# Layer 0 of a four-layer attention kernel: the next queries' norm in two steps on VectorE, three context steps ahead of cross attention's first pass, and two smaller staging tiles

## The chip, the cores and the metric

The kernel runs on one core of one Trainium2 chip. The metric is the device time of that core in microseconds (us): the median of three timed runs. One more run was taken with the hardware profiler; all times of single instructions come from it. Lines are told as L317, which is line 317 of the kernel before. Engines have the profile's names: PE is TensorE (PEld its weight load), DVE is VectorE, ACT is ScalarE, POOL is GpSimd, SP is the queue that issues the DMAs.

## The reference

Four layers work on x, 8 sequences of 256 tokens with 320 features, and on a context of 8 x 120 tokens with 192 features. The change lies in layer 0, and in the preparation of context keys and values for layers 1 to 3. Layer 0 is, cut to what matters:

```python
def attention(x, ctx, Wq, Wk, Wv, Wo, bo, heads):          # 20 heads of 16
    q, k, v = fq_sym(x @ Wq), fq_sym(ctx @ Wk), fq_sym(ctx @ Wv)   # 8-bit steps, one step for the whole tensor
    w = fq_zero(softmax(q k^T * dh ** -0.5))                       # 8-bit steps, one step for the whole tensor
    return (w v) @ Wo + bo

x = x + attention(layer_norm(x, ln1), layer_norm(x, ln1), Wq1, Wk1, Wv1, Wo1, bo1)   # self
x = x + attention(layer_norm(x, ln2), ctx, Wq2, Wk2, Wv2, Wo2, bo2)                  # cross
x = x + geglu_ff(layer_norm(x, ln3))
```

A quantisation step is taken from the maximum over a whole tensor (all batches), so each attention needs two passes over the scores: the first finds the sums of the softmax and from them the step of the weights, the second computes the weights again, rounds them to whole steps and multiplies them with the values. Layers 1 and 2 have cross attention to the same context with weights of their own, layer 3 too.

## The kernel before, in words

x stays in SBUF. A batch is one sequence of 256 tokens, as two tiles of 128. Heads go in groups, four heads to a group, and a "round" of the second pass handles one or two groups of a batch: five rounds make a batch.

The order of the work is written out by hand: generators are advanced in turn by `weave` (L651; each part has a round at which it starts), and `paced` (L663) lets a generator take a step only in every second round. Each engine then has one queue, in an order that the scheduler of the framework settles from this program order, from dependences and from its own estimate of times; an engine runs its queue strictly in that order. `behind` (L288) adds an order edge between two instructions of one engine, without a semaphore.

Self attention's second pass is `s.out_all()` (L1535). In each round, `weights` (L1565) calls `exps` (L1437): PE computes the scores of four heads into two PSUM pairs (L1454), ACT takes the exponential of each (L1461, tile `e`), and DVE rounds each to whole steps (L1569, tile `w`, from `e`). `e` and `w` share five buffers, so an exponential may have to wait for a rounding of the round before. PE multiplies the weights with the values two rounds later (L1551), DVE scales the result (`oTq`, L1561), and in two further rounds `project_out_steps` (L476) multiplies with Wo on PE (L120), after POOL has added the bias to x (`xb`, L481), and DVE adds the product into x (`x_sb`, L487). Meanwhile POOL rounds the values of the next batch (`whole_v`, L1355: `tv` at L1360, a memset at L1363, copies at L1369 and L1373).

Woven into this, from round 8 on, runs `c.queries_all()` (L1282): as soon as a batch of x is finished, its norm is taken (`normed`, L300: statistics, mean and variance, `ve` at L312 on DVE; rstd by a power at L314 on POOL; the two x-hat instructions at L317, one for each tile of 128 tokens), the result is transposed on PE (L334) and copied out by ACT with the norm's factors (`xT`, L342), and three matmul groups (L120) give cross attention's queries `Q`. In batches 1 to 6 the x-hat instructions are on POOL (`on=nc.gpsimd`), in batches 0 and 7 on DVE.

Cross attention begins with the quantisation steps (`c.steps()`), the rounding of the first batch's queries and keys (`c.whole(0, True)`, L1330), and then the first pass: `tops_all` (L1395) computes scores (L1410) in six units for each batch, and DVE takes their negated maximum (`negm`, L1413); `sums_all` follows two units behind the batch with exponentials and sums; `whole_all` rounds the next batch's queries and keys on POOL.

Woven into the first pass is `ahead`, which is `context_steps` (L702): 4 steps that compute layer 1's context keys for two batches each (`keys`, L754; PE 12 matmuls at L730, ACT copies them out into the staging tile `kst` at L364 and L368, and two DMAs write them to DRAM), then 4 steps of values (8 matmuls each, staging tile `vst`), then the same for layers 2 and 3. PSUM pairs for scores and for context steps come from the same pool of three. One step, with the loads of its weights, is taken right at the start, one after `c.steps()`, and up to 20 in the weave, one in two rounds; what is left runs beside the second pass of cross attention.

Of the kernel before, what the change touches and what calls it, by code (L numbers as in the profile page):

```python
# [11 lines left out]
F32 = mybir.dt.float32  # L12
BF16 = mybir.dt.bfloat16
AF = mybir.ActivationFunctionType
# [4 lines left out]
P = 128  # L19
B, N, C = 8, 256, 320  # L20
NT = B * N // P
TPB = N // P
# [11 lines left out]
G = H * PAD // P  # L34
# [3 lines left out]
G3 = H3 * PAD3 // P  # L38
T3 = 4
K3 = M - T3  # L40
# [14 lines left out]
class Kernel:  # L55
# [221 lines left out]
    def weight_o2(self, pool, name):  # L277
# [7 lines left out]
                    self.nc.sync.dma_start(w[r : r + D, g], src[h * D : (h + 1) * D])  # L285
        return w

    def behind(self, ins, last):  # L288

        if last is not None:  # L290
            order = mybir.DependencyInfo(mybir.DependencyClass.NoSync, mybir.DependencyReason.DATA)
            self.tc.add_manual_dep(ins.ins, last.ins.name, order, reason="order on the engine")
# [4 lines left out]
    def bank(self):  # L297
        return self.ps_a.tile([P, 512], F32, tag="a", name="pa")

    def normed(self, b, ln, on=None):  # L300

        nc = self.nc
        x = self.x[:, TPB * b : TPB * (b + 1), :]
        if ln is None:
            return x
        mv = self.small.tile([P, TPB, 2], F32, tag="mv", name="mv")
        for t in range(TPB):
            st = self.small.tile([P, 6], F32, tag="bnst", name="bnst")
            nc.vector.bn_stats(st, x[:, t, :])
            nc.vector.bn_aggr(mv[:, t, :], st)  # L310
        ve = self.small.tile([P, TPB], F32, tag="ve", name="ve")
        nc.vector.tensor_scalar(ve, mv[:, :, 1], EPS, None, ALU.add)  # L312
        rstd = self.small.tile([P, TPB], F32, tag="rstd", name="rstd")
        nc.gpsimd.tensor_tensor(rstd, ve, self.nhalf, ALU.pow)  # L314
        xh = self.work.tile([P, TPB, C], F32, tag="xh", name="xh")
        for t in range(TPB):
            (on or nc.vector).tensor_scalar(  # L317
                xh[:, t], x[:, t], mv[:, t, 0:1], rstd[:, t : t + 1], ALU.subtract, ALU.mult
            )
        return xh  # L320

    def turned(self, x, dst, at, ln=None, singles=False):

# [378 lines left out]
    def context_steps(self):  # L702
# [18 lines left out]
        wk = lambda n: weight("ck", n)  # L721
        wv = lambda n: weight("cv", n, 2)
        half = lambda i: slice(64 * i, 64 * (i + 1))

        def both(outs, whole, halves, more=False):

# [27 lines left out]
        def keys(name, w, k0, k1):  # L754
            k = k1 - k0
            for b in range(0, B, 2):
                ps = self.pair()
                keys_to(ps, w, ((0, (0, 1)), (2 * k, (2,))), slice(b, b + 2), k0, k1)
                st = pool.tile([P, 2, G, k], F32, tag="ks", name="kst")
                pv = ps[:, :, : 4 * k].rearrange("p i (m b k) -> p i m b k", m=2, b=2)  # L760
                for i in range(2):
                    self.put_k(st[:, i], pv[:, :, 0, i], pv[:, 0, 1, i])
                    nc.sync.dma_start(self.kd[name][:, b + i, :, k0:k1], st[:, i])
                yield

        w, w2 = wk("L1_xattn_k2"), wv("L1_xattn_v2")
# [24 lines left out]
        ps = self.pair()  # L791
        n = B * NIP
        keys_to(ps, w, ((0, (0, 1)), (n, (2,))), slice(0, B), NTXT, M)
        st = pool.tile([P, G, n], F32, tag="ks", name="kst")
        self.put_k(st, ps[:, :, :n], ps[:, 0, n : 2 * n], 1)
        for b in range(B):
            nc.sync.dma_start(self.kd["both"][:, b, :, NTXT:], st[:, :, b * NIP : (b + 1) * NIP])
# [12 lines left out]
        for b in range(0, B, 2):  # L810
            ps = self.pair()
            keys_to(ps, w, ((0, (0, 1)), (2 * K3, (2, 3))), slice(b, b + 2), 0, K3)
            st = pool.tile([P, 2, G3, K3], F32, tag="ks", name="kst")
            pv = ps[:, :, : 4 * K3].rearrange("p i (g b k) -> p g i b k", g=2, b=2)
            for i in range(2):
                for g in range(2):
                    nc.scalar.activation(
                        st[:, i, 2 * g : 2 * g + 2], pv[:, g, :, i], AF.Identity,
                        bias=self.cols[:, COL_ONE + 2 : COL_ONE + 3],
                    )  # L820
                nc.sync.dma_start(self.kd["last"][:, b + i], st[:, i])
            yield


# [361 lines left out]
class Quant:  # L1186
# [95 lines left out]
    def queries_all(self):  # L1282

        k, nc, w = self.k, self.k.nc, self.w
        x, xT = {}, {}

        def norm(b):
            x[b] = k.normed(b, self.ln, on=nc.gpsimd if 0 < b < B - 1 else None)

        def turn(b):  # L1290
            xT[b] = k.work.tile([P, 3, N], F32, tag="xT", name="xT")
            k.turned(x.pop(b), xT[b], 0, self.ln)
            self.q[b] = self.pool.tile([P, 3 * N], F32, tag="Q", name="Q", bufs=B)

        def project(b, m):
            ps = k.pair()
            k.mm(ps[:, 0, :N], [(w["q"][:, c, m * P : (m + 1) * P], xT[b][:, c, :]) for c in range(3)])
            nc.scalar.copy(self.q[b][:, m * N : (m + 1) * N], ps[:, 0, :N])
            if m == 2:
                self.top(0, b, self.q[b])  # L1300

        todo = {0: norm, 3: turn, 6: lambda b: project(b, 0), 7: lambda b: project(b, 1), 8: lambda b: project(b, 2)}
        for r in range(5 * B + 4):
            for b in range(B):
                if r - 5 * b in todo:
                    todo[r - 5 * b](b)
            yield
# [227 lines left out]
    def out_all(self):  # L1535

        k, nc, kc, ks = self.k, self.k.nc, self.kc, self.ks
        st = {}
        groups = [gs for gs, h in self.units if h == 0]
        rounds = len(groups)  # L1540

        def values(b, gs, w):
            for n, g in enumerate(gs):
                if g in (0, 4):
                    st["o"] = k.bank()
                o = st["o"]
                at = g // 2 % 2 * N
                for c in range(kc):
                    for j in range(4):
                        i = (n * kc + c) * N  # L1550
                        nc.tensor.matmul(  # L1551
                            o[j * PAD : (j + 1) * PAD, at : at + N], self.v[b][:ks, c, k.head(g, j), :],
                            w[:ks, j, i : i + N], start=g in (0, 4) and c == 0, stop=g in (3, 4) and c == kc - 1,
                            skip_group_check=True,
                        )
                if g in (3, 4):
                    if g == 3:
                        st["oT", b] = k.work.tile([P, 3, N], F32, tag="oT", name="oTq", bufs=1)
                    oT = st["oT", b]
                    dst = oT[:, :2, :] if g == 3 else oT[:, 2:, :]  # L1560
                    nc.vector.tensor_scalar(  # L1561
                        dst.rearrange("p c n -> p (c n)"), o[:, : dst.shape[1] * N], self.sc[:, 14:15], None, ALU.mult
                    )

        def weights(b, gs):  # L1565
            es, n = self.exps(b, gs, range(4), 1)
            w = self.pool.tile([P, 4, 512], BF16, tag="e", name="w", bufs=5)
            for i, e in enumerate(es):
                nc.vector.tensor_scalar(  # L1569
                    w[:ks, 2 * i : 2 * i + 2, :n], e[:ks, :, :n], MAGIC, MAGIC, ALU.add, ALU.subtract  # L1570
                )
            return w

        def project(b):
            yield from k.project_out_steps(b, st.pop(("oT", b)), self.w["o"], self.brow)

        for _ in self.whole_v(0):
            pass
        self.shift(0)
        todo, projects = [], {}  # L1580
        for r in range(rounds * B + 4):
            b, i = divmod(r, rounds)
            if b < B:
                w = weights(b, groups[i])
                if i == 0:
                    more = self.whole_v(b + 1) if b + 1 < B else iter(())
                todo.append((b, groups[i], w))
            if len(todo) > (2 if b < B else 0):
                values(*todo.pop(0))

            for t in range(TPB):
                d, left = divmod(r - 2 - t, rounds)
                if left == 0 and 1 <= d <= B:
                    if t == 0:
                        projects[d] = project(d - 1)
                        next(projects[d])
                    next(projects[d], None)
            if b < B:
                for _ in range(2):
                    next(more, None)  # L1600
                if i == rounds - 2 and b + 1 < B:
                    self.shift(b + 1)
            yield
# [3 lines left out]
def kernel(ctx: ExitStack, tc: tile.TileContext, a, out):  # L1607
    k = Kernel(ctx, tc, a, out)
    with ExitStack() as es:
# [15 lines left out]
        with tc.tile_pool(name="l0", bufs=1) as pool:  # L1625
# [24 lines left out]
            brow["ff0"] = k.bias_row(k.fk, 2)  # L1650
            w["self"], brow["self"] = load("L1", "q1", "k1", "v1", "o1_w", 3)
            c.steps()
            next(ahead)
            for _ in c.whole(0, True):
                pass
            n = len(c.units)
            k.weave(
                (0, c.tops_all()), (n + 4, c.sums_all()), (0, c.whole_all()), (5, v),
                (1, k.paced(islice(ahead, 20), 1)),
            )  # L1660
            c.weight_steps()

# [127 lines left out]
```

## Time and profile before

| | us |
|---|---|
| median of three timed runs | 2206.34 |
| the three runs | 2202.88, 2206.34, 2210.78 |
| the profiled run | 2212.34 |
| span of the profiled run, first to last instruction | 2210.5 |
| PE busy in it | 2041.3 (92%) |
| DVE, ACT, POOL busy in it | 1122.6, 822.9, 360.3 |
| self attention's second pass with the queries woven in | 257 to 412 |
| start of cross attention | 412 to 445 |
| cross attention's first pass | 445 to 543 |

Lines of the timeline are: start, duration, engine, line and operation, out<-in, shapes, xN for N instructions shown as one, and in brackets the idle time ahead of it on its engine with what ended it. The table by stretch gives busy time (and instructions) of each engine, then the granted clock of PE as a share of full speed, the DMA share and GB/s.

### The profile page before, as it was taken

Reading aid. Unit: us, or ns where it says so; the run is one execution under the profiler, and the core shown is the slowest. Engines: PE = TensorE matmul, PEld = TensorE weight load, DVE = VectorE, ACT = ScalarE, POOL = GpSimd, SP = SyncE. Lnnn points to the kernel's source line nnn. Section 1 sums busy time; section 2 is a strip of 40 time slices with the busy share of each in tenths; the row PEclk is TensorE's granted clock in tenths of the full one; section 3 lists DMA queues with packets and bytes.
Section 4 is the critical chain, followed back from the end, with each engine's and each line's share of the span. In section 5 each row is a group of like instructions: output and inputs, shape, how many; then the busy total and the mean of one; then the engine's idle time right before and its main releaser. Section 6 shows DMA issues by size and latency. Waiting matters only on the chain.

```text
span 2210.5 us, 38239 instructions
## 1 busy us (share of the span) xinstructions
PE 2041.3 (92%) x16413; PEld 1197.1 (54%) x16413; DVE 1122.6 (51%) x1695; ACT 822.9 (37%) x1249; POOL 360.3 (16%) x366
## 2 busy tenths in 40 slices
PE   6888889898899999999999999899999999999997
PEld 5643345554444555455555555545555655666664
DVE  4388687555742221335556566621121566546565
ACT  3347878467532121124444434321101333222221
POOL 1192056621411000000000010100000100000100
PEclk9989889899989999999999999999999999999999
DMA  4000000642111000020000001100000120000000
GB/s 118 17 12 2 1 1 1 172 112 57 55 47 51 1 0 1 1 93 2 2 2 22 27 25 36 46 2 0 0 1 1 24 64 26 18 18 26 23 19 16
DMA packets 79303, 63.21 MB, mean 29 GB/s; under 512 B 48410, under 2 KB 68318, under 8 KB 78622
## 3 DMA queue, kind: packets, MB, share of 16 engines
q1 hardware_dynamic: 75070, 57.06, 9.3%
q10 hardware_dynamic: 4064, 3.71, 0.6%
q8 instruction: 129, 2.11, 0.4%
q14 instruction: 40, 0.33, 0.1%
HBM read 42.61 MB, written 17.37 MB: 27 GB/s over the span
## 4 chain that ended last, share of the span: by engine, by line
PE 74%; DVE 17%; ACT 4%; issue 3%; DMA 1%; POOL 0%; ACTq 0%; SPq 0%; DVEq 0%; POOLq 0%
PE pf L588 13%; PE pf L120 13%; PE pf L132 9%; PE pa L120 7%; PE pa L451 6%; PE pf L434 4%; PE pa L588 3%; PE pf L139 3%; DVE negm L1413 3%; PE pf L389 3%; DVE rs L459 3%; PE pf L730 3%; PE pf L1454 2%; PE pa L1476 2%; DVE negm L396 2%
## 5 line engine op out<-in xcount | busy, mean ns | idle before, releaser
L440 ACT ACTIVATE e<-pf 128x1024 f32<-128x1024 f32 (+2 forms) x176 | 158.4, 945 | 219.2 <-PE pf L434 212.2
L396 DVE TENSOR_REDUCE negm<-pf 128x4 f32<-128x1024 f32 (+4 forms) x224 | 188.0, 885 | 97.1 <-PE pf L389 97.1
L588 PE MATMUL pf<-xTf,ff 128*128 128x512 f32 x512 | 232.5, 601 | 5.2 <-DVE negm L396 5.2
L459 DVE RECIPROCAL rs<-pa 128x256 f32<-128x256 f32 x88 | 152.2, 1745 | 143.6 <-PE pa L451 143.6
L1461 ACT ACTIVATE e<-pf,sc_s 128x1024 f32<-128x1024 f32 x160 | 169.4, 1117 | 55.0 <-PE pf L1454 45.8
L481 POOL TENSOR_TENSOR xb<-x_sb,brow 128x640 f32<-128x640 f32 x40 | 62.3, 1557 | 775.5 <-DVE x_sb L487 734.6
L613 DVE SCALAR_TENSOR_TENSOR hT<-pf,cols_sb,gl 128x512 f32<-128x512 f32 x64 | 47.9, 750 | 256.8 <-ACT gl L612 254.5
L1413 DVE TENSOR_REDUCE negm<-pf 128x4 f32<-128x1024 f32 (+2 forms) x128 | 143.4, 1133 | 63.5 <-PE pf L1410 56.7
L120 PE MATMUL pf<-ff,hT 128*128 128x320 f32 x640 | 174.4, 434 | 0.0
L588 PEld LDWEIGHTS pf<-xTf,ff 128*128 128x128 f32 x512 | 94.9, 191 | 125.3 <-issue 119.4
L120 PEld LDWEIGHTS pf<-ff,hT 128*128 128x128 f32 x640 | 120.9, 190 | 55.5 <-issue 6.1
L612 ACT ACTIVATE gl<-pf,cols_sb 128x512 f32<-128x512 f32 x64 | 43.9, 687 | 249.6 <-PE pf L588 249.6
L389 PE MATMUL pf<-kT,qT 32*128 32x120 f32 (+1 forms) x1920 | 111.8, 324 | 18.8 <-ACT e L440 18.5
L434 PE MATMUL pf<-qT,kT 32*128 32x256 f32 (+1 forms) x1280 | 119.8, 405 | 9.1 <-DVE negm L396 7.5
L120 PE MATMUL pa<-o,oT 128*128 128x320 f32 x352 | 105.7, 441 | 15.2 <-DVE oT L460 15.2
L1454 PE MATMUL pf<-Q,K 32*128 32x256 bf16 (+1 forms) x960 | 91.3, 294 | 24.7 <-DVE negm L1413 14.1
L389 PEld LDWEIGHTS pf<-kT,qT 32*128 32x128 f32 x1920 | 82.0, 185 | 59.1 <-ACT e L440 28.1
L641 POOL TENSOR_TENSOR xb<-x_sb,brow 128x640 f32<-128x640 f32 x16 | 25.2, 1575 | 542.6 <-DVE x_sb L646 527.9
L451 PE MATMUL pa<-e,v 128*32 128x256 f32 (+1 forms) x1280 | 105.6, 390 | 2.3 <-ACT e L440 1.7
L1569 DVE TENSOR_SCALAR w<-e 128x1024 bf16<-128x1024 f32 (+2 forms) x128 | 87.4, 692 | 32.1 <-ACT e L1461 31.0
L132 PE MATMUL pf<-xT,q 128*128 128x256 f32 x384 | 100.5, 391 | 0.4 <-ACT e L440 0.2
L1461 ACT ACTIVATE e<-pf,sc_c 120x1024 f32<-120x1024 f32 (+1 forms) x96 | 88.5, 981 | 31.6 <-PE pf L1454 28.8
(284 smaller groups left out, 3436.3 us busy)
## 6 DMA issues: line engine op xcount, KB each, us to landing
ff<-in_L_xattn_Wff_dram SPq DMA_DIRECT2D x1, 2560.0 KB
qT<-nT SPq DMA_DIRECT2D x160, 4.0 KB
ff<-in_L_xattn_ff_w_dram SPq DMA_DIRECT2D x1, 2560.0 KB
out_dram<-x_sb SPq DMA_DIRECT2D x16, 160.0 KB
kd_cross<-kst SPq DMA_DIRECT2D x8, 300.0 KB
vd_cross<-vst SPq DMA_DIRECT2D x8, 300.0 KB
vd_both<-vst SPq DMA_DIRECT2D x8, 300.0 KB
kT<-kd_cross SPq DMA_DIRECT2D x8, 300.0 KB
```

Of the source, the lines that this page charges most:

```text
L120: self.nc.tensor.matmul(out, l, r, start=i == 0, stop=i == len(pairs) - 1)
L132: self.nc.tensor.matmul(o, *t[c], start=start and c == 0, stop=stop and c == n - 1, skip_group_check=True)
L389: nc.tensor.matmul(s[j // 2][:, j % 2, o : o + nk], qT[r : r + PAD, g, t * P : (t + 1) * P], kT[r : r + PAD, g, :nk], start=True, stop=True,)
L396: nc.vector.tensor_reduce(negm[:, n, 2 * i : 2 * i + 2, g0 : g0 + len(gs), :].rearrange("p j g t -> p j (g t)"), sv[:, :, :, k0:k1], AX.X, ...
L434: nc.tensor.matmul(s[j // 2][:ks, j % 2, o : o + N], kT[r : r + PAD, g, c * ks : (c + 1) * ks], qT[r : r + PAD, g, :], start=True, stop=True,)
L440: nc.scalar.activation(e[:ks, 2 * i : 2 * i + 2, :n], s[i][:ks, :, :n], AF.Exp, scale=scale)
L451: nc.tensor.matmul(o[j * PAD : (j + 1) * PAD, what * N : (what + 1) * N], w, es[g][:ks, j, c * N : (c + 1) * N], start=first and c == 0 an ...
L459: nc.vector.reciprocal(rs, o[:, N:])
L588: ins = nc.tensor.matmul(*args, **kw)
L1413: nc.vector.tensor_reduce(negm[:, 2 * h : 2 * h + 2, gs[0] : gs[-1] + 1, :].rearrange("p j g t -> p j (g t)"), s[:, :, : len(gs) * TPB * n ...
L1454: nc.tensor.matmul(s[at // 2][:ks, at % 2, o : o + N], l, m, start=not shift and o == 0, stop=shift and o + N == n, skip_group_check=True,)
L1461: nc.scalar.activation(e[:ks, :, :n], ps[:ks, :, :n], AF.Exp, scale=self.sc[:ks, 9:10])
```

## The change

Three edits.

A. `normed` is split: `norm_steps` is a generator that first takes the statistics and rstd, and at its next step makes the two x-hat instructions, always on DVE. `queries_all` takes the two steps in rounds 5b and 5b + 1 of a batch. The x-hat of the first tile gets an order edge behind the last rounding `w` that has been written at that point (`k.last_w`); the x-hat of the second tile gets none. In the compiled order of DVE this gives, for batches 1 to 6: `ve`, x-hat of the second tile, `w`, `w`, x-hat of the first tile, `oTq`; for batch 0: `w`, x-hat, `w`, x-hat, where before it was x-hat, x-hat, `w`, `w`.

B. After `c.steps()` three context steps are taken instead of one, so the steps with keys 2, 3 and 4 of layer 1 are written ahead of cross attention's first scores; the weave takes 18 instead of 20. On PE 12 + 12 matmuls at L730 move ahead of the first L1410, and the later context steps move up by two places.

C. The staging tile for keys held both batches of a step in one buffer; now each batch has a tile of its own out of two buffers. Each batch's DMA was its own before, too.

```diff
@@ def normed
-    def normed(self, b, ln, on=None):
+    def normed(self, b, ln):
...
+        steps = self.norm_steps(b)
+        next(steps)
+        return next(steps)
+
+    def norm_steps(self, b):
+
+        nc = self.nc
+        x = self.x[:, TPB * b : TPB * (b + 1), :]
...
         nc.gpsimd.tensor_tensor(rstd, ve, self.nhalf, ALU.pow)
+        yield
         xh = self.work.tile([P, TPB, C], F32, tag="xh", name="xh")
         for t in range(TPB):
-            (on or nc.vector).tensor_scalar(
+            self.last_norm = nc.vector.tensor_scalar(
                 xh[:, t], x[:, t], mv[:, t, 0:1], rstd[:, t : t + 1], ALU.subtract, ALU.mult
             )
-        return xh
+            if t == 0 and self.norm_behind is not None:
+                self.behind(self.last_norm, self.norm_behind)
+        yield xh
@@ def context_steps
+        staged = lambda g, n: pool.tile([P, g, n], F32, tag="ks", name="kst", bufs=2)
...
-                st = pool.tile([P, 2, G, k], F32, tag="ks", name="kst")
                 pv = ps[:, :, : 4 * k].rearrange("p i (m b k) -> p i m b k", m=2, b=2)
                 for i in range(2):
-                    self.put_k(st[:, i], pv[:, :, 0, i], pv[:, 0, 1, i])
-                    nc.sync.dma_start(self.kd[name][:, b + i, :, k0:k1], st[:, i])
+                    st = staged(G, k)
+                    self.put_k(st, pv[:, :, 0, i], pv[:, 0, 1, i])
+                    nc.sync.dma_start(self.kd[name][:, b + i, :, k0:k1], st)
...
@@ def queries_all
+        def stats(b):
+            x[b] = k.norm_steps(b)
+            next(x[b])
+
         def norm(b):
-            x[b] = k.normed(b, self.ln, on=nc.gpsimd if 0 < b < B - 1 else None)
+            k.norm_behind = k.last_w
+            x[b] = next(x[b])
+            k.norm_behind = None
...
-        todo = {0: norm, 3: turn, 6: lambda b: project(b, 0), 7: lambda b: project(b, 1), 8: lambda b: project(b, 2)}
+        todo = {0: stats, 1: norm, 3: turn, 6: lambda b: project(b, 0), 7: lambda b: project(b, 1), 8: lambda b: project(b, 2)}
@@ def weights in out_all
-                nc.vector.tensor_scalar(
+                k.last_w = nc.vector.tensor_scalar(
                     w[:ks, 2 * i : 2 * i + 2, :n], e[:ks, :, :n], MAGIC, MAGIC, ALU.add, ALU.subtract
                 )
@@ tile_xattn_kernel
             c.steps()
-            next(ahead)
+            for _ in range(3):
+                next(ahead)
             for _ in c.whole(0, True):
                 pass
...
-                (1, k.paced(islice(ahead, 20), 1)),
+                (1, k.paced(islice(ahead, 18), 1)),
```

The third use of the staging tile, layer 3's keys, is split in the same way.

## The prediction, made before the changed kernel was run

> **What bounds the kernel now.** I read the chain of work that ended last, then the busy table by stage, then the engine timelines of the two places that the change touches. All times are of the profiled execution: span 2210.5 us, run 2212.34 us, which is 6.0 us above the median of the three timed runs (2206.34; 2202.88 to 2210.78). The chain:
>
> ```profile
> PE 74%; DVE 17%; ACT 4%; issue 3%; DMA 1%; POOL 0%; ACTq 0%; SPq 0%; DVEq 0%; POOLq 0%
> ```
>
> TensorE (PE) bounds the kernel, GpSimd (POOL) has no share. The stages are self attention's second pass (257 to 412), the start of cross attention (412 to 445) and its first pass (445 to 543):
>
> ```profile
> 257.00:412.00 155.00, 135.81 (x1290) 81.33 (x1289) 117.93 (x231) 115.42 (x151) 75.91 (x68) 0.89 0.12 31
> 412.00:445.00 33.00, 24.84 (x152) 13.65 (x152) 16.73 (x27) 11.89 (x42) 33.00 (x29) 0.74 0.57 165
> 445.00:543.00 98.00, 93.29 (x1044) 48.13 (x1043) 47.46 (x88) 71.49 (x119) 10.75 (x8) 0.98 0.35 85
> ```
>
> Columns: stretch, length, busy PE, weight loads, VectorE, ScalarE, GpSimd, granted clock, DMA. The first pass is PE's (93.29 of 98). Its start is not: there PE has gaps and a clock of 0.74.
>
> **Part A, the norm.** Batches 1 to 6 lose two GpSimd x-hats (L317) and gain two on VectorE; batches 0 and 7 were on VectorE already. In the steady stretch a batch takes 15.6 us (x_sb at 333.30, then 348.90), of which PE is busy 14.12, ScalarE 13.5, GpSimd 12.4, VectorE 12.08. GpSimd, VectorE and ScalarE around one norm, each from its own timeline:
>
> ```profile
> 338.99 1.16 POOL L314 TENSOR_TENSOR rstd<-ve,nhalf 128x2 f32<-128x2 f32 x1
> 340.25 3.42 POOL L317 TENSOR_SCALAR xh<-x_sb,mv,rstd 128x320 f32<-128x320 f32 x2
> 343.66 1.22 POOL L1360 TENSOR_SCALAR tv<-V,sc_s 128x640 f32<-128x640 f32 x1
> ```
>
> ```profile
> 338.04 0.88 DVE L312 TENSOR_SCALAR ve<-mv 128x2 f32<-128x2 f32 x1
> 338.82 1.28 DVE L1569 TENSOR_SCALAR w<-e 128x1024 bf16<-128x1024 f32 x2
> ```
>
> ```profile
> 339.52 2.12 ACT L1461 ACTIVATE e<-pf,sc_s 128x1024 f32<-128x1024 f32 x2 [0.24 <-PE pf L1454]
> ```
>
> What is removed bought nothing on the path: GpSimd ends x-hat at 343.66, and the transposes that read it start at 343.96 without a wait. What is added lies on the path. In the compiled order of the changed kernel only the first tile's x-hat is held behind the weight roundings w; the second tile's has no such edge and stands right behind ve, ahead of both w. So VectorE's queue stops there for rstd, with the two w behind it, and the exponential whose buffer the first w frees (the second of the 2.12 pair, due at 339.52 + 1.12 = 340.64) behind those; PE's next scores wait for that exponential.
>
> How late is the first w? rstd alone takes 0.715 us (shortest of eight; 1.16 beside w): 338.99 + 0.71 = 339.70. From there GpSimd goes straight to tv (L1360) and the memset (L1363). Batch 0 of before shows such a meeting:
>
> ```profile
> 290.09 0.79 POOL L1360 TENSOR_SCALAR tv<-V,sc_s 128x640 f32<-128x640 f32 x1
> 290.94 1.22 POOL L1363 MEMSET V<- 128x1280 bf16 x1
> ```
>
> ```profile
> 290.13 2.22 DVE L317 TENSOR_SCALAR xh<-x_sb,mv,rstd 128x320 f32<-128x320 f32 x2 [0.61 <-POOL rstd L314]
> 292.27 1.37 DVE L1569 TENSOR_SCALAR w<-e 128x1024 bf16<-128x1024 f32 x2
> ```
>
> The x-hat pair took 2.22 us there, against 0.80 us in batch 7, where GpSimd had nothing to do; its end, 292.35, lies just behind the memset's, 292.16. [...] By this row the first w ends 339.70 + about 2.6 (tv 0.8, memset 1.2, the rest of w 0.5) = 342.3, 1.7 us past 340.64. By the uncontended row it ends 338.92 + 0.78 (rstd) + 0.44 (x-hat) + 0.69 (w) = 340.87, 0.2 late. I take 1.7: it is the same pair of instructions beside the same x-hat. ScalarE runs almost without gap from 339.52 until PE's only wait of the period (1.25 us for xT), so nothing absorbs it.
>
> Sum of A: batches 1 to 4 have tv and memset there: 4 x 1.7 = 6.8 (0.8 by the other end). Batch 5 has none: 0.2. Batch 6: 0, since its first w ends at 387.5 either way by the wait on the residual row. Batch 7: 0, same engine and a PE-bound tail. Batch 0 gains: there both w stood behind both x-hats, PE waited 3.6 us and ScalarE 4.6 us for the first; now it goes ahead (2.4 earlier) and the second 0.9 earlier. I take -1.5, between -2.4 and 0. Stall: **+5.5** (-1.4 to +7).
>
> The clock. Granted clock goes down in steps of 3.41 us, and one such stretch after 636.76 to 640.17 fell to half although PE's longest gap in it was 0.76 us: it held almost only 32-row matmuls (L1454, L1551). A stretch with 1.54 us idle but 128-row matmuls (L120) on both sides, 384.2 to 387.6, kept full speed. With the stall, some 2.9 us lie between two L120 groups (341.4 to 344.3), with 32-row work alone. One halved stretch doubles about 1.7 us of PE work. I take about one such in four batches, **+2** (0 to +7, if all four fall).
>
> [...]
>
> **Part B, three context steps ahead, and C, the staging tiles.** The start of cross attention on PE:
>
> ```profile
> 414.68 0.47 PE L1410 MATMUL pf<-K,Q 32*128 32x120 bf16 x16 [2.25 <-DVE Q L1353]
> 416.35 4.96 PE L730 MATMUL pf<-ctxT,ck 128*128 128x240 f32 x12 [1.20 <-DVE negm L1413]
> ...
> 423.08 4.96 PE L730 MATMUL pf<-ctxT,ck 128*128 128x240 f32 x12 [1.23 <-DVE negm L1413]
> ```
>
> PE waits 2.25 us for Q, the clock falls at 414.90, and steps 3 and 4 run at half speed, 4.96 us each; the step at 407.17 took 2.58 us. The granted clock is back at 431.97, five stretches later. After: step 3 fills 412.43 to about 414.9, step 4 to 417.3, both at full clock, so tops begin at 417.3, 2.6 us later than now. SP's queue issues the same keys' transfers, only earlier, ahead of value weights that are used later. Steps 3 and 4 hold two of three PSUM pairs until ScalarE has copied them out, and each copy waits for its staging tile's transfer (about 3 us from 411.25), so the scores start with one pair and pace themselves by negm (1.1 to 1.2 us each): second at 418.95, the first value step at 420.6. Between 417.3 and 420.6 there is only 32-row work, so I expect one or two halved stretches here in place of five, and batch 1's scores at about 433.6, where they are now (433.59). But two context steps more are done by then: 2 x 2.05 us (a value step at full clock is 8 matmuls, 2.0 to 2.07 us) leave the PE-bound pass. ScalarE (71.49 of 98) becomes the next bound in the rounds left without them, so not quite all counts: **-4**. If the clock holds: tops of batch 1 at 432.1, -5.6; if two stretches more fall: -0.7. GpSimd is full there (33.00 of 33), but Q of batch 1 was ready at 419.1, long before use. C lets a copy wait for one transfer, not both: 0 (-0.5 to +0.3), part of B.
>
> **Sum.** +5.5 + 2 - 4 = +3.5 us: 2216 against the profiled run, **2209.8** against the median.
>
> **Rivals.**
> 1. Faster: the engines don't collide (rstd later or earlier than tv's start), and the clock holds at cross attention's start. A -1.4, B -5.6: 2199.3. For: the row of 0.80 us. Against: the row of 2.22 us.
> 2. Slower: the stall also drops the clock in every one of batches 1 to 4. [...] A +5.5 + 7, B -4: 2214.8; with B at -0.7, 2218. For: the stretch at 636.76. Against: the stretch at 384.2.
> 3. B gives nothing: held PSUM pairs and the chain of copy and transfer give back what the filled gap gains. A +7.5, B about 0: 2213.8. For: transfers of 3 us, one after the other. Against: PE has value steps to do meanwhile.
> 4. The norm is not where its order edge wants it. That is so for one tile of two, and is in the forecast.
>
> **How the numbers follow.** Differences under 0.3% (6.6 us) can hardly be told from none here. Forecast (2203 to 2213): 0.50; rival 1: 0.20; rival 2: 0.20; rival 3: 0.10. Below 2199.7 lie half or more of rival 1 and a little of the forecast: 0.19. Above 2213 lie most of rivals 2 and 3 and a little of the forecast: 0.30. Between: 0.51. The range runs from rival 1 with a little more gain, 2197, to rival 2 with B at its weak end and a little over, 2220.
>
> **What would show it.** A: VectorE with idle before x-hat "<- POOL rstd", x-hat near 1 us or more in batches 1 to 4 and 0.45 in 5 and 6; "PE L1454 <- ACT e" or "ACT e <- DVE w" of 1.7 us in four periods; a period of 17.3 in place of 15.6, or over 18.5 where the clock fell. B: no 2.25 us gap before the first L1410; steps 3 and 4 at 2.4 to 2.6 us; fewer halved stretches between 412 and 432. Wrong would be a period still of 15.6 to 15.9, or halved clock from 415 on as now.

## The result, and the profile after

| | before | changed | ratio, 95% interval |
|---|---|---|---|
| first measurement (4 runs each) | 2208.56 | 2234.72 (2222.09 to 2239.30) | 1.0104, 1.0078 to 1.0129 |
| second, on another occasion (35 and 12 runs) | 2210.57 | 2226.27 (2216.50 to 2236.66) | 1.0051, 1.0028 to 1.0075 |
| profiled run of the first | 2212.34 | 2236.02 | |

The changed kernel is slower: 23 us by the first measurement, 11 us by the second, which has three times the runs. Here and below, microseconds of gain or loss are taken from the ratio as it is on record, which is not the quotient of the two medians (these lie 26.2 and 15.7 us apart). Forecast were +3.5 us, with 2220 as the upper end.

In the views from here on, line numbers are those of each run's own kernel. In the changed kernel rstd is L324, x-hat L328, the exponentials L1481, the roundings w L1589, self attention's scores L1474, the context matmuls L744, cross attention's first scores L1430, negm L1433, tv L1380 and the memset L1383; in the other kernels they lie a few lines away.

The chain of waits of the changed kernel still belongs to PE:

```profile
PE 74%; DVE 16%; ACT 5%; issue 3%; DMA 1%; POOL 1%; SPq 0%; ACTq 0%; DVEq 0%; POOLq 0%
```

The busy table of the changed kernel, cut at the places that answer to 257, 412, 445 and 543 (columns as before: stretch, length, busy PE, weight loads, VectorE, ScalarE, GpSimd, granted clock, DMA, GB/s):

```profile
259.10:424.40 165.30, 139.61 (x1290) 83.40 (x1288) 125.71 (x242) 116.25 (x151) 57.22 (x56) 0.88 0.11 29
424.40:459.40 35.00, 28.48 (x176) 16.05 (x177) 18.10 (x28) 15.16 (x54) 35.00 (x30) 0.80 0.72 199
459.40:559.20 99.80, 94.27 (x1024) 46.37 (x1022) 47.37 (x88) 68.77 (x108) 8.88 (x7) 0.88 0.29 68
```

Self attention's second pass is 10 us longer. The first pass of cross attention should have lost two context steps; instead it is longer, and its granted clock went from 0.98 to 0.88. GpSimd gave up 18.7 us in the first of the stages, and nothing came of it.

To compare kernels I cut each trace at instructions that all of them have (the ends of the first and last weight rounding of self attention, and of the first and last negm of cross attention's first pass). "Half clock" is a granted clock of 0.5. In us, with the part spent at half clock in brackets:

| profile | second pass of self | from there to the first cross scores | first pass of cross |
|---|---|---|---|
| before | 123.9 (30) | 26.6 | 111.1 (19) |
| changed, first profile | 134.2 (37) | 29.3 | 112.1 (38) |
| changed, second (kernel 5 below) | 130.1 (28) | 29.3 | 121.7 (55) |
| changed, third (kernel 11 below) | 134.0 (37) | 29.3 | 106.4 (17) |

Of the 23.5 us between the first two profiles, 10.3 lie in the second pass of self attention, 2.7 + 1.0 in the next two columns, 2.1 ahead of the change and 7.5 behind layer 0's attention, in code that the change does not touch (35 us at half clock there in place of 17). So nearly 10 us of that pair of profiles lie outside the stages that the change touches, where the changed kernel's run spent more time at half clock. In the second profile of the changed kernel the same stretch took 1551.6 us, as before (1551.5).

The norm of one batch in the changed kernel, from GpSimd's, VectorE's and ScalarE's timelines:

```profile
345.93 0.72 POOL L324 TENSOR_TENSOR rstd<-ve,nhalf 128x2 f32<-128x2 f32 x1
346.64 0.80 POOL L1380 TENSOR_SCALAR tv<-V,sc_s 128x640 f32<-128x640 f32 x1
347.50 1.22 POOL L1383 MEMSET V<- 128x1280 bf16 x1
```

```profile
344.98 0.87 DVE L322 TENSOR_SCALAR ve<-mv 128x2 f32<-128x2 f32 x1
346.69 0.93 DVE L328 TENSOR_SCALAR xh<-x_sb,mv,rstd 128x320 f32<-128x320 f32 x1 [0.83 <-POOL rstd L324]
347.54 2.42 DVE L1589 TENSOR_SCALAR w<-e 128x1024 bf16<-128x1024 f32 x2
```

```profile
346.46 1.11 ACT L1481 ACTIVATE e<-pf,sc_s 128x1024 f32<-128x1024 f32 x1 [0.24 <-PE pf L1474]
349.36 1.11 ACT L1481 ACTIVATE e<-pf,sc_s 128x1024 f32<-128x1024 f32 x1 [1.79 <-DVE w L1589]
```

Here is the chain that was forecast, link for link: VectorE idles 0.83 us for rstd, with the pair of w in its queue behind x-hat (the exponentials that the pair reads had ended at 345.86), x-hat takes 0.93 us beside tv, the pair of w takes 2.42 us in place of 1.28 with the memset beside it (347.50 to 348.72), and the second exponential starts 1.79 us late. PE, whose time counts, waits for it, as its timeline shows between two batches' transposes (L347):

```profile
335.31 0.82 PE L347 MATMUL pf<-ident,xh 128*128 128x128 f32 x6
...
350.53 0.29 PE L1474 MATMUL pf<-Q,K 32*128 32x256 bf16 x3 [1.87 <-ACT e L1481]
...
352.80 0.82 PE L347 MATMUL pf<-ident,xh 128*128 128x128 f32 x6
```

From batch to batch (start of the transposes) it is 17.49 us where the clock holds, against 15.60.

The start of cross attention on PE:

```profile
423.35 6.51 PE L744 MATMUL pf<-ctxT,ck 64*128 64x240 f32 x32
429.80 0.38 PE L1430 MATMUL pf<-K,Q 32*128 32x120 bf16 x8
431.43 0.39 PE L1430 MATMUL pf<-K,Q 32*128 32x120 bf16 x8 [1.25 <-DVE negm L1433]
433.07 2.69 PE L744 MATMUL pf<-cv,ctxT 128*120 128x320 f32 x8 [1.25 <-DVE negm L1433]
...
438.26 3.84 PE L744 MATMUL pf<-cv,ctxT 128*120 128x320 f32 x8 [0.15 <-ACT kst L381]
```

The gap of 2.25 us is gone and the steps ahead run at full clock (32 matmuls in 6.51 us). The clock falls later, at 434.33, and then the value steps pay: 3.84 us, against 1.97 at full clock in the kernel before.

### The profile page after: what moved, and what is told of

It reads as the page before. It is cut to its first block, busy times and chain, and to the rows that moved or that the text cites. A ratio compares the mean times of both kernels' runs of the same rounds, so it can differ in the third digit from the quotient of the medians.

```text
span 2234.0 us, 38241 instructions
## 1 busy us (share of the span) xinstructions
PE 2062.8 (92%) x16413; PEld 1204.7 (54%) x16413; DVE 1131.0 (51%) x1707; ACT 824.4 (37%) x1249; POOL 341.3 (15%) x354
## 4 chain that ended last, share of the span: by engine, by line
PE 74%; DVE 16%; ACT 5%; issue 3%; DMA 1%; POOL 1%; SPq 0%; ACTq 0%; DVEq 0%; POOLq 0%
PE pf L601 13%; PE pf L120 12%; PE pf L132 9%; PE pa L120 7%; PE pa L464 6%; PE pf L447 4%; PE pa L601 3%; PE pf L1474 3%; PE pf L139 3%; PE pf L402 3%; DVE negm L1433 3%; DVE rs L472 3%; PE pa L1496 2%; PE pf L744 2%; DVE negm L409 2%
## 5 line engine op out<-in xcount | busy, mean ns | idle before, releaser
L1481 ACT ACTIVATE e<-pf,sc_s 128x1024 f32<-128x1024 f32 x160 | 170.2, 1117 | 62.7 <-PE pf L1474 47.3
L1433 DVE TENSOR_REDUCE negm<-pf 128x4 f32<-128x1024 f32 (+2 forms) x128 | 143.7, 1134 | 72.6 <-PE pf L1430 60.6
L120 PE MATMUL pf<-ff,hT 128*128 128x320 f32 x640 | 174.4, 434 | 0.0
L120 PEld LDWEIGHTS pf<-ff,hT 128*128 128x128 f32 x640 | 120.9, 190 | 55.5 <-issue 6.1
L1474 PE MATMUL pf<-Q,K 32*128 32x256 bf16 (+1 forms) x960 | 93.7, 304 | 30.8 <-ACT e L1481 12.1
L120 PE MATMUL pa<-o,oT 128*128 128x320 f32 x352 | 107.3, 446 | 15.2 <-DVE oT L473 15.2
L1589 DVE TENSOR_SCALAR w<-e 128x1024 bf16<-128x1024 f32 (+2 forms) x128 | 90.4, 718 | 31.5 <-ACT e L1481 31.0
L1481 ACT ACTIVATE e<-pf,sc_c 120x1024 f32<-120x1024 f32 (+1 forms) x96 | 88.2, 980 | 38.0 <-PE pf L1474 35.7
```

The costliest lines, as they stand in the source:

```text
L120: self.nc.tensor.matmul(out, l, r, start=i == 0, stop=i == len(pairs) - 1)
L1433: nc.vector.tensor_reduce(negm[:, 2 * h : 2 * h + 2, gs[0] : gs[-1] + 1, :].rearrange("p j g t -> p j (g t)"), s[:, :, : len(gs) * TPB * n ...
L1474: nc.tensor.matmul(s[at // 2][:ks, at % 2, o : o + N], l, m, start=not shift and o == 0, stop=shift and o + N == n, skip_group_check=True,)
L1481: nc.scalar.activation(e[:ks, :, :n], ps[:ks, :, :n], AF.Exp, scale=self.sc[:ks, 9:10])
```

## The experiments

My theory: A costs by the stall at the head of VectorE's queue and by the clock that goes with it; B gains at the start, and loses it again when the clock falls later in the first pass. The rival: the loss is in the context steps or the staging tiles and in later stages. Every kernel was timed beside the kernel before on the same chip; ratios are against that. Kernels 1 to 8 ran on one chip, 9 to 12 on another.

**1. The norm alone (A).** Context steps and staging tile as before.

> The norm's part alone (A): the norm in two steps on VectorE, with context steps and staging tile as before. Theory 1 (the stall at the head of VectorE's queue, with the clock that it costs): second pass of self attention about 10 us longer, as in the changed kernel, so about 2219 us (2213 to 2224) against 2208.6, x-hat of the second tile near 0.93 us in batches 1 to 4, periods of 17.4 to 18.3 us there. Theory 2 (most of the loss comes from the context steps or the staging tiles and shows in later stages): at most +7, 2215 or less, and nothing lost behind 675 us.

2221.81 us against 2212.66, ratio 1.0031 (1.0010 to 1.0051): 2 to 11 us. In its profile the second pass of self attention takes 131.2 us, 7.3 more, at the same half clock (31 us); periods are 17.55, 17.49, 18.01 us. Behind layer 0's attention it is 3.8 us longer, with 28 us at half clock in place of 17; the third kernel, whose norm costs nothing, shows the same there, so that is not A. The time alone does not part the two theories, since theory 2 allowed up to +7 us; the place of the loss and the periods do. So theory 1 holds for A, at the lower end of its size.

**2. The context steps and the tiles alone (B and C).**

> Three context steps ahead and the two staging tiles alone (B and C), the norm as before. Theory 1: between a gain of 4 us and a loss of 5 us, 2204 to 2213, the loss only if the clock falls late in cross attention's first pass, where no context steps are left to raise it again. Theory 2: 2220 us or more, with the loss behind 445 us.

2215.87 us, ratio 1.0016 (0.9992 to 1.0040), that is +3.5 us. The rival's 2220 is not reached, but no gain is seen either. In its profile the first pass takes 117.9 us, of which 44 at half clock.

**3. The order edge on both x-hats.** A alone, with

```diff
-            if t == 0 and self.norm_behind is not None:
+            if self.norm_behind is not None:
```

> The norm's part alone, with the order edge on both tiles' x-hats, so that both roundings stand ahead of both x-hats. Theory 1: VectorE still waits for rstd but with no rounding behind it in that time, so the 1.7 us stalls go and batch 0 gains 1 to 2 us: 2204 to 2210 us, period 15.6 to 16. Rival (not the order but the meeting of x-hat on VectorE with tv and the memset on GpSimd costs, wherever x-hat stands): periods of 16.5 us or more, 2212 us or more.

2212.67 us, ratio 0.9995 (0.9972 to 1.0019). Periods are 15.66 to 15.73 us and the second pass takes 122.7 us. VectorE's timeline at the same place:

```profile
338.49 0.87 DVE L322 TENSOR_SCALAR ve<-mv 128x2 f32<-128x2 f32 x1
339.28 1.28 DVE L1588 TENSOR_SCALAR w<-e 128x1024 bf16<-128x1024 f32 x2
340.63 2.15 DVE L328 TENSOR_SCALAR xh<-x_sb,mv,rstd 128x320 f32<-128x320 f32 x2
```

The pair of x-hats still meets tv and the memset (2.15 us), but behind both w, where nobody waits for it long. The absolute time is one that the rival allowed, but the kernel before took 2212.66 us beside it; the periods, far from the rival's 16.5, decide. So the order decides, and the missing edge on the second tile is all of A's loss that can be measured.

**4. The context steps later in the weave.** B and C, with

```diff
-                (1, k.paced(islice(ahead, 18), 1)),
+                (5, k.paced(islice(ahead, 18), 1)),
```

> As the second kernel of this call (B and C alone), but the paced context steps of the weave begin at round 5, not 1, so that they end as late as in the kernel before. Theory 1: the late fall of the clock is as rare as before, 2203 to 2208 us. Rival (what B loses is lost at its start, through PSUM pairs and staging): the same as without the shift, within 2 us.

2205.76 us, ratio 0.9962 (0.9942 to 0.9981): 8 us faster, more than I expected. First pass 101.9 us, of which 10 at half clock. Cut at the changes of its clock:

```profile
412.00:419.98 7.98, 6.73 (x48) 4.55 (x47) 4.29 (x10) 4.22 (x11) 7.42 (x6) 1.00 0.76 224
419.98:430.22 10.24, 7.17 (x44) 3.79 (x37) 7.70 (x11) 4.67 (x12) 10.24 (x11) 0.50 0.75 188
430.22:539.44 109.22, 101.59 (x1126) 52.76 (x1123) 57.31 (x103) 77.76 (x143) 28.39 (x25) 1.00 0.37 93
```

After 430.22 the clock is never at half for 109 us, to beyond the end of the first pass. Less work falls into the slow part at the start, too: PE is busy for 7.17 us in it, against 11.51 in the changed kernel's first profile (434.33 to 447.98). Kernels 2 and 4 differ in nothing but the round at which the weave's context steps start, and their intervals do not meet: part B is worth having, and the start at round 1 takes it away.

**5. The changed kernel again.**

> The changed kernel once more, beside the others on one chip. The two parts alone gave +6.8 us (A, interval 2 to 11) and +3.5 us (B and C, interval -2 to +9). Theory 1 (the parts add up, and what the first runs showed above that is the clock in stages that the change does not touch, which differs from run to run): +7 to +14 us against before. Rival (the parts harm each other, for example by the moment at which the first pass starts): +19 us or more, as in the first runs.

Ratio 1.0051 (1.0028 to 1.0075), +11.3 us: the parts add up (6.9 + 3.5) within their intervals. Its profile has the longest half-clock stretch that any of the profiles has in the first pass. The busy table, cut at the clock's changes:

```profile
436.64:453.71 17.07, 14.00 (x114) 8.51 (x114) 12.09 (x21) 8.22 (x30) 17.07 (x15) 1.00 0.65 180
453.71:491.26 37.55, 37.44 (x219) 19.26 (x218) 10.70 (x16) 17.29 (x33) 8.35 (x7) 0.50 0.30 67
```

For 37.55 us PE is busy throughout (37.44) and stays at half clock all the same. The context steps in that stretch, from PE's timeline:

```profile
460.71 4.43 PE L744 MATMUL pf<-ctxT,ck 128*128 128x208 f32 x12
...
470.48 4.43 PE L744 MATMUL pf<-ctxT,ck 128*128 128x208 f32 x12
...
479.24 3.84 PE L744 MATMUL pf<-cv,ctxT 128*120 128x320 f32 x8
...
486.90 3.85 PE L744 MATMUL pf<-cv,ctxT 128*120 128x320 f32 x8
```

The fall at 453.71 comes when exponentials are added to the scores (their matmuls, L1474, start at 450.07). In the kernel before the clock falls there as well, at 445.62 (L1454 from 443.22), and is back after one stretch of 3.41 us, which a value step fills (the first line is a value step at full clock):

```profile
437.98 1.97 PE L730 MATMUL pf<-cv,ctxT 128*120 128x320 f32 x8
445.58 3.71 PE L730 MATMUL pf<-cv,ctxT 128*120 128x320 f32 x8
```

Here the value steps have already been used up, because all steps moved two places ahead, and key steps follow.

I counted the half-speed stretches of 3.41 us in the first pass in all fourteen profiles: of 29 with key steps and neither value steps nor much else of 128 rows (up to 3.41 us of key matmuls in one) not one was followed by full speed; of 27 with 2.2 us or more of value matmuls 21 were (23 of 35 with 1.5 us or more). One left out of the 29, with 1.97 us of key matmuls beside 1.65 us of L120, was followed by full speed. In the kernel before a stretch in which PE was busy throughout with a value step (445.62 to 449.03, 3.41 of 3.41 us) was followed by full clock; a stretch full of key steps, as at 470.8 to 474.2 here, was not: busy was not enough here. That the kind of step decides is argued from these counts; what in the key steps (208 columns or 240, against 320, for one) makes the difference was not tried.

**6. Both mendings.** The changed kernel with the edits of 3 and 4.

> The changed kernel with both mendings: the order edge on both tiles' x-hats, and the paced context steps from round 5 on. Theory 1: 0 of A and -8 of B: 6 to 10 us faster than before. Rival (what the late start gained was one chip's clock): within 3 us of before.

2205.12 us, ratio 0.9962 (0.9941 to 0.9982), the same gain as the fourth kernel: the mended norm is worth nothing measurable, the context steps 8 us. First pass 101.1 us.

**7. tv later.** A alone, and tv waits for a copy on VectorE that is ordered behind a later rounding:

```diff
+            sv = k.small.tile([P, 1], F32, tag="sv", name="sv")
+            k.behind(nc.vector.tensor_copy(sv, sc[:, 8:9]), k.last_w)
-            nc.gpsimd.tensor_scalar(tv[:ks, :kc], v[:ks, :kc], sc[:ks, 8:9], MAGIC, ALU.mult, ALU.add)
+            nc.gpsimd.tensor_scalar(tv[:ks, :kc], v[:ks, :kc], sv[:ks], MAGIC, ALU.mult, ALU.add)
```

> The norm's part alone, with its single edge, but tv (and with it the memset) made to wait for a small copy on VectorE that stands two roundings later, so that GpSimd is idle while x-hat runs. If the meeting of x-hat with tv and memset is what makes the stall long: x-hat at 0.45 us, the first rounding 0.2 us late instead of 1.8, periods of 15.6 to 16.0 us, 0 to +3 us against before. If the wait for rstd at the head of VectorE's queue alone does it: periods of 17 us or more, +6 us or more.

Ratio 1.0004 (0.9982 to 1.0026). VectorE's timeline:

```profile
344.03 0.45 DVE L328 TENSOR_SCALAR xh<-x_sb,mv,rstd 128x320 f32<-128x320 f32 x1 [0.84 <-POOL rstd L324]
344.39 1.29 DVE L1593 TENSOR_SCALAR w<-e 128x1024 bf16<-128x1024 f32 x2
```

The wait for rstd is there as in the changed kernel (0.84), the meeting is not: x-hat 0.45, the pair of w 1.29. The period is 15.95 us. That splits the 1.89 us of a batch: 0.35 for standing at the head of the queue, 1.54 for the meeting with tv and the memset that this brings about. The time is that of the kernel before within the interval, so the split is the profile's.

**8. The tiles alone (C).** Only the staging tile is split.

> The two staging tiles alone (C), context steps and norm as before. Theory 1: within 3 us of before. Rival (the tiles change how copies wait for transfers and so shift the late fall of the clock): more than 4 us either way.

Ratio 1.0001 (0.9976 to 1.0027); first pass 109.9 us. Nothing, as forecast.

**9. A start between.** As 4, with round 3 in place of 5.

> B and C alone, with the paced context steps from round 3 on: between the start at 1 (+3.5 us, with 24 us at half clock behind the first exponentials) and the start at 5 (-8 us, with none). In rounds 3 to 9 stand the four value steps, in rounds 11 to 17 the four key steps of layer 2, and the exponentials begin at round 10. Theory 1a (a fall of the clock at the first exponentials lasts until a value step comes, so what counts is which steps follow round 10): like the start at 1, a half-speed stretch of more than 10 us after the first exponentials if the clock falls there at all, -2 to +5 us against before. Theory 1b (what counts is only how late the last context step stands): half way, -2 to -5 us, and no long half-speed stretch early.

Ratio 0.9992 (0.9970 to 1.0013), first pass 112.3 us with 31 at half clock, but in three stretches of 6.8 us behind the first exponentials and none over 10. That fits neither expectation well and does not tell the two apart.

**10 and 11. Two more profiles**, of B and C alone and of the changed kernel, one run each.

> B and C alone as changed, one more profile. Theory 1a: again a half-speed stretch of more than 10 us somewhere between the first exponentials and the end of the first pass, as in three profiles of three with this order; the five profiles with the order of before have at most 3.4 us there. Rival (chance): none.

> The changed kernel, one more profile, for the same question and for the periods of the norm: 17.5 us in batches 1 to 4 where the clock holds, and a half-speed stretch of more than 10 us in cross attention's first pass.

2206.65 and 2216.81 us. Both have only 3.4 us at half clock behind the first exponentials, and first passes of 106.5 and 106.4 us. So I was wrong in "again": a long stretch came in three of the five profiles with the changed order of steps, and in none of the eight with the order of before or the start at 5 (before, 1, 3, 4, 6, 7, 8, 12), which have at most 3.4 us at a time behind the first exponentials. The changed kernel itself has such a stretch in two profiles and none in the third, so when the clock falls is not the order of steps alone. The two profiles without it are those of the second chip: chance and chip are not told apart. That the order decides how long it stays down is my reading of the counts under 5. Of the norm's periods in the last profile, 17.54 us is the expected one; in those of 18.29 and 19.09 the clock fell for 3.41 us. The first, 20.48, begins in a half-clock stretch that the kernel before has there too (18.47).

**12. The later start alone.** The kernel before with the weave's context steps from round 5 (20 steps, none moved ahead).

> The kernel before with one edit: the paced context steps of the weave start at round 5, not 1; no step is moved ahead, the tiles are as before. Theory 1 (the start at 5 lets the three steps ahead pay; without them the gap of 2.25 us before the first scores and the fall of the clock stay, and the last context steps only move later): -3 to +3 us against before, granted clock at half from about 415 us on. Rival (the late start alone makes the 8 us of the fourth and the sixth kernel): 6 us or more faster.

2209.49 us, ratio 1.0003 (0.9981 to 1.0026). PE's timeline has the old gap, and behind it the clock is down: four matmuls at L120 take 2.49 us at 418.55, 1.34 us at 424.59. The gap:

```profile
413.53 0.61 PE L1410 MATMUL pf<-K,Q 32*128 32x120 bf16 x16 [2.24 <-DVE Q L1353]
```

Its first pass takes 111.7 us. So the 8 us of kernels 4 and 6 need both: three steps ahead, and the rest late.

## Why the prediction was wrong

**A was right.** Forecast +7.5 us (stall 5.5, clock 2), measured +6.9 (2 to 11), and 6.2 to 10.3 in the profiles. The first rounding was taken as 1.7 us late, and the exponential was 1.79 late, 1.89 a batch. Batch 5, without tv, was put at 0.2 and took 0.36. Batch 0 gained 0.9 (27.6 us from its first rounding to its transposes, against 28.5), where 1.5 was taken. The choice of the row with the meeting (2.22 us for the pair in batch 0) over the uncontended one (0.80) was what made this right, and the seventh kernel (without the meeting 0.45 us for x-hat and 1.29 for the pair of w) shows that the meeting was the cause. That tv, the memset and the rest of w add up was my estimate from that one row; in the changed kernel x-hat ended 0.18 us behind tv, the pair of w 1.24 us behind the memset. The clock fell once more, for 3.41 us, in two of the four batches of the first profile and of the third, and in none of the second: as rival 2 had it in part. Two slips changed nothing: the uncontended sum is 340.83, not 340.87; and of the matmuls called 32-row, L1551 works on 120 or 128 rows and 32 columns (form 120*32), only L1454 on 32 rows.

**The step that failed is B's -4**, with "I expect one or two halved stretches here in place of five" and "two context steps more are done by then". Measured is +3.5 (-2 to +9). The start itself came as forecast: the scores begin 2.7 us later (2.6 forecast), and the first value step 3.27 us behind them (3.3). Three things were off. Three to five stretches were halved at the start in the five profiles (10.2 to 17.1 us), not one or two, and value steps ran in them at up to 3.85 us in place of 1.97. Where the clock held afterwards, the way from the last rounding to the end of the first pass (the two right-hand columns of the table) took 135.6 and 135.7 us against 137.7: the gain was 2, not 4. And in three of five profiles the clock fell once more and was down for 24 to 44 us in all, which made them 141.4, 147.0 and 151.0 us. The mean of the five lies 4.4 us above the kernel before, which agrees with the timed +3.5 (four more profiles with the step order of before, kernels 1, 3, 7 and 8, have 136.7 to 138.0). I had counted the moved steps as time that leaves a PE-bound pass, and had not asked what the clock does at the place they leave; the fourth kernel, which puts the rest of the steps back to late rounds, has 10 us at half clock in its first pass, against 44 in the second kernel's profile, and gains the 8 us. Rival 3 had B's sum nearer and the reason wrong: the fourth kernel has the same PSUM pairs, copies and tiles and gains.

**The range** was also too narrow at its upper end: it counted the clock only in the two places that the change touches, while the first pair of profiles differs by 9.6 us in code that the change does not touch. Of the 20 us by which the first pair of profiles exceeds the forecast, about 8 are B's, 3 are A's, and nearly 10 lie in those stages. That part I take for luck: the eighth kernel, which cost nothing, is 7 us longer in the same code behind layer 0 in its profile. Why the first measurement lies 12 us above the second I can show only for its profile (9.6 us in stages with unchanged code); for the other three runs it stays open.

## What to carry to other kernels

Before an instruction is put on another engine, look which one the scheduler puts ahead of it and behind it: an order edge on one of two sister instructions leaves the other free to go to the head of the queue, and what then waits behind it is the price (here an exponential 1.79 us late), not its own 0.45 us. When work is moved to fill a gap, ask what runs in its old place, and what the clock does there: here the first pass was at half clock for 44 us in the profile of kernel 2, with the rest of the steps from round 1, and for 10 us in that of kernel 4, with them from round 5. Compare several profiles before a few us are put down to an edit, and compare them stage by stage with the half-clock time beside each.

## What the runs showed of the hardware

- Matmuls with a side of 32 (L1410 and L1454 work on 32 rows, L1476 on 120 rows and 32 columns), with 0.56 us of small transposes among them, kept the full clock once it was there (517 to 539 us in the kernel before, clock 1.00, PE busy 20.98 of 22.00). In the first profile of the changed kernel, with almost only such work behind a fall, it stayed at half for seven stretches of 3.41 us (519.66 to 543.56): the first held the end of the last context step (1.87 us of value matmuls), and of the six others only the last was followed by full clock. In the ninth kernel one such stretch (531.62 to 535.04) was followed by full clock as well. Just ahead of the fall in the changed kernel ScalarE waited 2.79 us for a transfer and PE 1.52 us for ScalarE. From the timeline of all engines, and the busy table after it:

```profile
516.50 0.36 ACT L820 ACTIVATE vst<-ident 128x192 f32<-128x192 f32 x1 [2.79 <-DMA vd_both<-vst]
...
518.08 0.43 PE L1474 MATMUL pf<-Q,K 32*120 32x256 bf16 x4 [1.52 <-ACT kst L381]
```

```profile
480.00:519.66 39.66, 36.77 (x414) 19.18 (x413) 20.62 (x35) 26.11 (x42) 0.00 (x0) 1.00 0.34 85
519.66:543.56 23.90, 23.24 (x258) 9.68 (x256) 13.55 (x20) 12.44 (x18) 0.00 (x0) 0.50 0.20 39
```

- A VectorE instruction of 0.45 us took 0.93 when GpSimd had started 0.05 us ahead of it, and the two roundings behind it 2.42 in place of 1.29. The roundings began 0.04 us behind the memset and ended 1.24 us after it (348.72, 349.96), near the 1.29 that they take alone. x-hat ended only 0.18 us after tv (347.44, 347.62), less than its own 0.45, so part of it ran beside tv.
- Single runs of one kernel spread over 20 us and more: 2216.50 to 2236.66 for the changed one, with a granted clock of 0.969 in the shortest and 0.958 in the longest.
